# Picked k and v rows: one masked tile and four products in the edge values' bank, in place of two tiles and eight products in the query bank

## The chip, the cores and the metric

One core of one Trainium2 chip. The metric is the device time of one execution in microseconds, the median of the runs shown. Profiles are single executions taken with the hardware profiler.

## The reference

A layer of a graph network over 6250 nodes and 206250 edges, 64 channels in 4 heads of 16, and a residual layer norm behind it:

```python
Qh = (x @ Wq.T + bq).reshape(n, H, D)
Kh = (x @ Wk.T + bk).reshape(n, H, D)
Vh = (x @ Wv.T + bv).reshape(n, H, D)
Ee = (edge_attr @ We.T + be).reshape(-1, H, D)
score = (Kh[src] * Qh[dst] * (1.0 / np.sqrt(D)) * Ee).sum(-1)
score = jnp.exp(jnp.clip(score, -5.0, 5.0))
msg = Vh[src] * score[..., None]
wV = jax.ops.segment_sum(msg, dst, num_segments=n)
x = _layernorm(x + wV.reshape(n, H * D))
```

The edges are sorted by `dst`; all values are float32.

## The kernel before

A tile is 128 edges, a group 8 tiles; there are 202 groups. A first stage computes tables of k and v and of q for all nodes and writes them to DRAM. The main loop then goes over the groups, one round for each, and its order is written out by hand: within a round the instructions of each engine are queued as the code states them, and an engine takes its queue in order. The waits between engines are put in by the framework from what tiles are written and read.

In round g the parts are these. `edges(g + 3)` multiplies edge attributes with `We` into the PSUM tile `ee`. `biased(g + 2)` on ACT adds the bias and copies `ee` to SBUF as `eb`. `queries(g + 2)` puts the q of each edge into the PSUM tile `qq` by a product with a one-hot of the destinations. `terms(g + 1)` on DVE multiplies `eb` with `qq`; `turn(g + 1)` transposes the result on PE into `qe`. `products` and `weigh` make the scores of g on DVE and ACT, `message` and `keep`/`take` the messages, and `sums` (PE) adds the messages of a step of two groups into `pa`, from where `add` (DVE, L900 first) takes them a round later.

k and v of the sources come from the table by indirect DMAs on GpSimd (L295), a DMA for each tile. For two tiles of a group, of 156 groups, they are made on the core: a **batch** is four such tiles (two groups of two), and there are 78 batches. Batches last three and two groups in turn. Over a batch, `hots` (DVE, partly widened by ACT) makes one-hots of the source rows, and `picks` (PE, 50 matmuls in a batch) selects with them from all of x, held in SBUF. x lies there four nodes to a row, so that a pick bank holds two nodes' 64 channels, one in the upper and one in the lower 64 partitions: `px[0]` for the first two of the four and `px[1]` for the other two. `odd` (DVE, L259) is the source index modulo 4 and says which of the four is meant. At the end of a batch `picked` (DVE, L722 and L723) copies each bank to SBUF, masked by `odd`; the next batch's first picks write the same banks. In the round after, `biased_kv` (ACT, L733) fills the bank of `qq` with the bias, `picked_kv` (PE) adds the products of both masked tiles with `w2`, the weights of k and v, and `place_kv` (ACT, L739) copies k and v to the place where a gather would have put them. `queries(g + 2)` follows in that bank, last but one in this round's PE queue; in other rounds it stands behind `turn`.

`READY` holds the last round of each batch, `BEGIN` the first. All matmuls but the turns are issued by one helper (L744), so PE's groups are told apart by tiles. The PSUM tile `room` takes two of the eight banks: one half is `ee`, the other holds `pa` and `folded`.

Of the kernel before, what the change touches and what calls it, by code (L numbers as in the profile page):

```python
# [8 lines left out]
F32 = mybir.dt.float32  # L9
BF16 = mybir.dt.bfloat16  # L10
I32 = mybir.dt.int32
U8 = mybir.dt.uint8
# [137 lines left out]
def tile_gnn(ctx: ExitStack, tc: tile.TileContext, x, x_blocks, by_rows, xT, wT, bias, beT, weT, eT, src, src_rows,  # L150
# [502 lines left out]
    with tc.If(rv == 0) as branch:  # L653

        with tc.tile_pool(name="work", bufs=2) as work, \
# [7 lines left out]
            nc.tensor.transpose(col, row_b[:, 0:1].to_broadcast([P, P]), ident_b)  # L663
            nc.tensor.transpose(still[:, C:C + UNITS].bitcast(BF16),
                                half_b[:2 * UNITS].to_broadcast([2 * UNITS, P]), ident_b[:2 * UNITS, :2 * UNITS])
            room = fixed.tile([P, 2, 4 * P], F32, name="room")
            ee = room[:, 0].rearrange("p (i e) -> p i e", e=P)
            pa = room[:, 1, :2 * PA]
            folded = room[:, 1, 2 * PA:2 * PA + 2 * C].rearrange("p (b c) -> p b c", c=C)
            sum_ = still[:, 2 * P:2 * P + C]  # L670
            px = [fixed.tile([P, 4 * P], F32, name=f"pick{k}") for k in range(2)]
            xs = [accp.tile([P, 4 * P], F32, name=f"x{k}") for k in range(2)]
            qq = fixed.tile([P, G // 2, P], F32, name="qq")
            qe = [fixed.tile([P, G, C], F32, name=f"qe{k}") for k in range(2)]

            rooms = qq.rearrange("p i e -> p (i e)").rearrange("p (j c) -> p j c", j=BATCH)

            def pairs(ap):

# [39 lines left out]
            def picked(m):  # L719

                odd = ODD.pop(m)
                nc.vector.scalar_tensor_tensor(xs[0], odd, upper, px[0], op0=OP.is_equal, op1=OP.mult)  # L722
                nc.vector.scalar_tensor_tensor(xs[1], odd, upper2, px[1], op0=OP.is_equal, op1=OP.mult)  # L723

            def picked_kv(m):
                for j in range(BATCH):
                    for k in range(2):
                        product(rooms[:, j], xs[k][:, j * P:(j + 1) * P], w2, start=False,
                                stop=k == 1 and j == BATCH - 1, skip_group_check=True)

            def biased_kv(m):

# [10 lines left out]
            def product(*aps, **kw):  # L743
                mark.append(nc.tensor.matmul(*aps, **kw))  # L744
# [6 lines left out]
            def biased(g):  # L751

                n = tiles_of(g) // 2
                EB[g] = work.tile([P, G // 2, P], F32, name="eb")
                nc.scalar.activation(EB[g][:, :n], ee[:, :n], AF.Identity, bias=be_col)  # L755
# [258 lines left out]
            for g in range(NG + 1):  # L1014
# [37 lines left out]
                    add(s)  # L1052
                if g - 1 in FOLDS:
                    add_blocks(FOLDS[g - 1])
                if g - 1 in READY:
                    biased_kv(READY.index(g - 1))
                if g + 2 < NG:
                    biased(g + 2)
                for piece in ahead[:1]:
                    hots(*piece)  # L1060
                if now:
# [23 lines left out]
                for k in range(max(len(todo), 3)):  # L1085
                    for one in todo[k:k + 1]:
                        picks(*one)
                        where.append(mark[-1])
                    if k == 1:
                        if g + 1 < NG:  # L1090
                            turn(g + 1)
                        if g - 1 in READY:
                            picked_kv(READY.index(g - 1))
                            place_kv(READY.index(g - 1))
                        elif g + 2 < NG:
                            queries(g + 2)
                    if k in (2, 4) and short and g not in READY:
                        short.pop(0)()
                while short:
                    short.pop(0)()  # L1100
                if g + 2 < NG and g - 1 in READY:
                    queries(g + 2)
                if g + 3 < NG:
                    edges(g + 3)
                where.append(mark[-1])
# [18 lines left out]
                    take(g, 0)  # L1124
                if g in READY:
                    picked(READY.index(g))
                if done:

                    while closed < B - 2 and summed[closed] <= g:
# [192 lines left out]
```

## Time and profile before

| | |
|---|---|
| median of 3 runs | 1998.6 us (1994.48 to 2001.87) |
| the profiled execution | 2019.47 us |
| its span, first to last instruction | 2017.7 us |
| mean granted clock of TensorE | 0.932 |
| ACT busy | 1328.1 us, 66% |
| GpSimd (POOL) busy | 1255.5 us, 62% |
| DMA, mean over the span | 101 GB/s |

The profiled execution is 1% above the median of the runs. Busy times are read against the span. Names in the profile are those of tiles: `pick` the banks `px`, `qq<-w,x` the products of the picked rows, `qq<-to,qw` the query products, `room<-et` the edge products, `room<-msg` the sums, `still` the tile that holds the sum taken out.

### The profile page before, as it was taken

To read this page: it belongs to the slowest core of one execution; us is meant where nothing else is said; L and a number is where in the kernel's file an instruction comes from. 1 tells how busy PE (TensorE), PEld (TensorE's weight loads), DVE (VectorE), ACT (ScalarE), POOL (GpSimd) and SP (SyncE) were. 2 spreads that over 40 slices of the span, in tenths; PEclk is the share of its full clock that TensorE was granted. 3 is DMA by queue.
4 is the path that set the end of the run, shared out by engine and by line. 5 is a ranking of instruction groups with operands and counts; after the bars stand their busy time and mean duration, and the time that the engine had idled before them with its cause. 6 is when DMAs were issued, how large, how long until landed. Compare 5 with 4: busy or idle time off the path is not lost.

```text
span 2017.7 us, 25692 instructions
## 1 busy us (share of the span) xinstructions
PE 1738.5 (86%) x7993; PEld 1259.1 (62%) x7993; DVE 1486.0 (74%) x2650; ACT 1328.1 (66%) x2047; POOL 1255.5 (62%) x1310
## 2 busy tenths in 40 slices
PE   6569989888888898979888989888888988889995
PEld 6346666666666665657566666666666666656664
DVE  5457777777777686878777777778777777678786
ACT  3456676676766676767667667667766667577674
POOL 6566666666666665666666666666666666666441
PEclk9789999999999998999899999999989999999996
DMA  6523333333333333333333333333333333333320
GB/s 178 190 90 114 100 103 103 98 97 100 93 108 101 91 102 88 102 115 99 93 97 92 107 104 93 104 90 103 101 88 114 104 95 104 97 93 98 97 71 20
DMA packets 116116, 203.70 MB, mean 101 GB/s; under 512 B 54784, under 2 KB 56425, under 8 KB 115855
## 3 DMA queue, kind: packets, MB, share of 16 engines
q1 hardware_dynamic: 73932, 116.94, 19.0%
q0 software_dynamic: 41600, 83.97, 14.7%
q10 hardware_dynamic: 436, 1.04, 0.2%
q8 instruction: 65, 1.06, 0.2%
q14 instruction: 83, 0.68, 0.1%
HBM read 194.25 MB, written 7.59 MB: 100 GB/s over the span
## 4 chain that ended last, share of the span: by engine, by line
PE 63%; DVE 16%; issue 7%; ACT 6%; another core or an unknown queue 4%; DMA 2%; POOL 1%; DVEq 0%; SPq 0%; ACTq 0%; POOLq 0%
PE pick L744 37%; PE room L744 10%; PE qq L744 10%; PE qe L775 4%; DVE hot L696 3%; DMA kv<-kv_tab,src_i 2%; DVE score L808 2%; DVE prod L806 1%; DVE qe L830 1%; DVE x L722 1%; DVE term L769 1%; POOL kv L295 1%; ACT kv L739 1%; DVE msg L850 1%
## 5 line engine op out<-in xcount | busy, mean ns | idle before, releaser
L295 POOL DMA_INDIRECT kv<-kv_tab,src_i x1260 | 1216.2, 965 | 708.8 <-issue 277.1
L744 PE MATMUL pick<-hot,parts 128*128 128x512 f32 x3900 | 1143.6, 436 | 115.5 <-DVE x L722 79.5
L744 PEld LDWEIGHTS pick<-hot,parts 128*128 128x128 f32 x3900 | 742.3, 198 | 418.8 <-issue 167.8
L696 DVE TENSOR_TENSOR hot<-from,still 128x1024 fp32r<-128x1024 bf16 x231 | 280.3, 1213 | 0.6 <-ACT from L257 0.6
L707 ACT ACTIVATE hot<-thin 128x1024 fp32r<-128x1024 bf16 x234 | 245.4, 1049 | 19.4 <-remote 19.3
L769 DVE TENSOR_TENSOR term<-eb,qq 128x512 f32<-128x512 f32 x202 | 137.3, 680 | 137.2 <-PE qq L744 98.1
L755 ACT ACTIVATE eb<-room,be_col 128x512 f32<-128x512 f32 x202 | 137.1, 679 | 148.2 <-DVE still L900 50.4
L744 PE MATMUL room<-et,we_sb 128*128 128x512 f32 x404 | 226.2, 642 | 7.5 <-ACT eb L755 6.2
L844 ACT ACTIVATE msg<-qe 128x512 fp32r<-128x512 f32 (+1 forms) x206 | 123.2, 598 | 157.5 <-DVE qe L830 74.4
L278 ACT ACTIVATE to<-to,one_p 126x1024 bf16<-126x1024 bf16 x198 | 225.7, 1140 | 0.1
L272 ACT ACTIVATE to<-kb,minus_row 126x1024 bf16<-126x1024 uint8 x198 | 225.2, 1137 | 0.0
L813 ACT ACTIVATE score<-score,five_p 128x32 f32<-128x32 f32 x203 | 64.1, 316 | 235.4 <-DVE score L808 144.6
L775 PE MATMUL qe<-ident,term 128*128 128x128 f32 x806 | 135.5, 294 | 58.9 <-DVE term L769 39.4
L775 PEld LDWEIGHTS qe<-ident,term 128*128 128x128 f32 x806 | 104.0, 151 | 111.9 <-DVE term L769 55.8
L744 PE MATMUL qq<-w,x 128*128 128x128 f32 x1248 | 165.8, 288 | 5.0 <-issue 3.6
L806 DVE TENSOR_TENSOR prod<-kv,qe 128x512 f32<-128x512 f32 x203 | 137.0, 675 | 43.1 <-remote 38.3
L830 DVE SCALAR_TENSOR_TENSOR qe<-weight,kv 128x512 f32<-128x512 f32 x200 | 139.8, 699 | 35.1 <-ACT weight L815 22.3
L722 DVE SCALAR_TENSOR_TENSOR x<-odd,upper,pick 128x512 f32<-128x512 int32 x77 | 57.3, 744 | 144.7 <-PE pick L744 115.2
L744 PEld LDWEIGHTS qq<-w,x 128*128 128x128 f32 x1248 | 155.6, 202 | 12.9 <-issue 8.0
L696 DVE TENSOR_TENSOR thin<-from,still 128x1024 bf16<-128x1024 bf16 x231 | 157.1, 680 | 0.0
L808 DVE TENSOR_REDUCE score<-prod 128x32 f32<-128x512 f32 x203 | 138.5, 682 | 7.0
L850 DVE TENSOR_TENSOR msg<-qe,msg 128x512 fp32r<-128x512 f32 x194 | 132.2, 681 | 2.9 <-ACT msg L844 1.4
(166 smaller groups left out, 1490.5 us busy)
## 6 DMA issues: line engine op xcount, KB each, us to landing
et<-in_eT SPq DMA_DIRECT2D x100, 512.0 KB
kb<-key_tab SPq DMA_DIRECT2D x101, 252.0 KB
kv<-kv_tab,src_i POOLq DMA_INDIRECT x1260
srcs<-in_src_rows SPq DMA_DIRECT2D x78, 256.0 KB
qw<-q_tab SPq DMA_DIRECT2D x202, 15.8 KB
kv_tab<-kv_sb SPq DMA_DIRECT2D x4, 640.0 KB
q_tab<-q SPq DMA_DIRECT2D x5, 480.0 KB
out<-y SPq DMA_DIRECT2D x2, 512.0 KB
```

The source lines that it names most:

```text
L272: nc.scalar.activation(TO[g][:, :n, :], KB.pop(g)[:, :n * P].rearrange("p (j e) -> p j e", j=n), AF.Square, bias=minus_row3[:3 * W])
L278: nc.scalar.activation(TO[g][:, :n, :], TO[g][:, :n, :], AF.Relu, bias=one_p[:3 * W], scale=-1.0)
L295: return nc.gpsimd.indirect_dma_start(out=kv_of(g)[:, j, :], out_offset=None, in_=kv_tab[:, :], in_offset=bass.IndirectOffsetOnAxis(ap=src ...
L696: nc.vector.tensor_tensor(to.rearrange("p b (a c) -> p b a c", c=2), pairs((FROM if hi < UNITS else OVER)[m])[:, None].to_broadcast(shape) ...
L707: nc.scalar.activation(*THIN.pop(0), AF.Copy)
L744: mark.append(nc.tensor.matmul(*aps, **kw))
L769: nc.vector.tensor_mul(TERM[g][:, :n], EB.pop(g)[:, :n], qq[:, :n])
L775: nc.tensor.transpose(qe[g % 2][:, 2 * k:2 * k + 2, :], TERM[g][:, k, :], ident)
L806: nc.vector.tensor_mul(prod, kv_of(g)[:, lo:hi, :C], qe[g % 2][:, lo:hi, :])
L808: nc.vector.tensor_reduce(SCORE[g], prod.rearrange("p g (h d) -> p g h d", h=H), axis=AX.X, op=OP.add)
L830: nc.vector.scalar_tensor_tensor(to.rearrange("p g (h d) -> p g h d", h=H), WEIGHT.pop(g)[:, :, :, None].to_broadcast([P, n, H, D]), LEAST ...
L850: nc.vector.tensor_sub(part_of(g, 1)[1], left, part)
```

## The change

The two masked tiles become one. The first bank is copied under its mask as before, which leaves zeros where the second is meant; there the second bank is copied over it with a predicated copy, whose mask, a tile of bytes `second`, is made by a new DVE instruction in the round that begins a batch. One tile means four products with the weights, not eight. `ee` and the rest of `room` become tiles of their own, and the products of the picked rows go to `ee`'s bank, no longer to that of `qq`. For that `biased_kv` comes behind `biased(g + 2)`, which empties `ee`, and `queries(g + 2)` stands behind `turn` in every round.

```diff
-            room = fixed.tile([P, 2, 4 * P], F32, name="room")
-            ee = room[:, 0].rearrange("p (i e) -> p i e", e=P)
-            pa = room[:, 1, :2 * PA]
-            folded = room[:, 1, 2 * PA:2 * PA + 2 * C].rearrange("p (b c) -> p b c", c=C)
+            ee = fixed.tile([P, G // 2, P], F32, name="ee")
+            room = fixed.tile([P, 4 * P], F32, name="room")
+            pa = room[:, :2 * PA]
+            folded = room[:, 2 * PA:2 * PA + 2 * C].rearrange("p (b c) -> p b c", c=C)
...
-            xs = [accp.tile([P, 4 * P], F32, name=f"x{k}") for k in range(2)]
+            xs = accp.tile([P, 4 * P], F32, name="x0")
+            SECOND = {}
+
+            def second(m):
+
+                SECOND[m] = work.tile([P, BATCH * P], U8, name="second")
+                nc.vector.tensor_scalar(SECOND[m], ODD[m], upper2, None, op0=OP.is_equal)
...
-            rooms = qq.rearrange("p i e -> p (i e)").rearrange("p (j c) -> p j c", j=BATCH)
+            rooms = ee.rearrange("p i e -> p (i e)").rearrange("p (j c) -> p j c", j=BATCH)
...
-                nc.vector.scalar_tensor_tensor(xs[0], odd, upper, px[0], op0=OP.is_equal, op1=OP.mult)
-                nc.vector.scalar_tensor_tensor(xs[1], odd, upper2, px[1], op0=OP.is_equal, op1=OP.mult)
+                nc.vector.scalar_tensor_tensor(xs, odd, upper, px[0], op0=OP.is_equal, op1=OP.mult)
+                nc.vector.copy_predicated(xs, SECOND.pop(m), px[1])
...
                 for j in range(BATCH):
-                    for k in range(2):
-                        product(rooms[:, j], xs[k][:, j * P:(j + 1) * P], w2, start=False,
-                                stop=k == 1 and j == BATCH - 1, skip_group_check=True)
+                    product(rooms[:, j], xs[:, j * P:(j + 1) * P], w2, start=False, stop=j == BATCH - 1,
+                            skip_group_check=True)
...
+                if g + 2 < NG:
+                    biased(g + 2)
                 if g - 1 in READY:
                     biased_kv(READY.index(g - 1))
-                if g + 2 < NG:
-                    biased(g + 2)
...
                         if g + 1 < NG:
                             turn(g + 1)
+                        if g + 2 < NG:
+                            queries(g + 2)
                         if g - 1 in READY:
                             picked_kv(READY.index(g - 1))
                             place_kv(READY.index(g - 1))
-                        elif g + 2 < NG:
-                            queries(g + 2)
...
-                if g + 2 < NG and g - 1 in READY:
-                    queries(g + 2)
...
+                if g in BEGIN:
+                    second(BEGIN.index(g))
```

On PE, in the first round of a batch of three groups, from the last product of the picked rows (`qq<-w`) to the edge products (`room<-et`), before the change:

```order
L744 MATMUL qq<-w_100,x_760 128x128
L744 MATMUL pick_757<-hot,parts 128x512 x2
L744 MATMUL pick_758<-hot,parts 128x512 x2
L744 MATMUL pick_757<-hot,parts 128x512 x2
L744 MATMUL pick_758<-hot,parts 128x512 x2
L744 LDWEIGHTS qw [waits DMAHW6_49]
L744 MATMUL qq<-to,qw 64x512 [waits Activation_49]
L744 LDWEIGHTS qw
L744 MATMUL qq<-to,qw 64x512
L744 MATMUL room<-et,we_sb 128x512 [waits DMAHW2_49,DVE_49]
```

and in the same round of the changed kernel, from the query products to the edge products (now `ee<-et`):

```order
L749 LDWEIGHTS qw [waits DMAHW6_49]
L749 MATMUL qq<-to,qw 64x512
L749 LDWEIGHTS qw
L749 MATMUL qq<-to,qw 64x512
L749 MATMUL ee<-w_100,x_760 128x128 [waits Activation_49]
L749 MATMUL ee<-w_100,x_760 128x128 x3
L749 MATMUL pick_758<-hot,parts 128x512 x2
L749 MATMUL pick_759<-hot,parts 128x512 x2
L749 MATMUL pick_758<-hot,parts 128x512 x2
L749 MATMUL pick_759<-hot,parts 128x512 x2
L749 MATMUL ee<-et,we_sb 128x512 [waits DMAHW2_49,Activation_49]
```

The query products moved from behind eight picks to ahead of the products of the picked rows, of which there are four; the edge products, which waited for DVE, wait for ACT, and the wait of the queries for ACT is gone.

On ACT, in the same kind of round, from the fill with the bias (`qq<-bkv_all`) to the copies of k and v, before:

```order
L733 ACTIVATE qq<-bkv_all 128x512 [waits DVE_49,PE_49]
L755 ACTIVATE eb<-room,be_col 128x512 [waits DVE_49,PE_49]
L844 ACTIVATE msg<-qe_763 128x8x64 [waits DVE_49]
L272 ACTIVATE to<-kb,minus_row_86 126x1024
L707 ACTIVATE hot<-thin 128x1024 [waits DVE_49]
L739 ACTIVATE kv_68<-qq 128x256 [waits PE_49,Activation_49]
L739 ACTIVATE kv_68<-qq 128x256
```

and in the changed kernel:

```order
L760 ACTIVATE eb<-ee,be_col 128x512 [waits PE_49]
L738 ACTIVATE ee<-bkv_all 128x512 [waits Activation_49]
L849 ACTIVATE msg<-qe_763 128x8x64 [waits DVE_49]
L272 ACTIVATE to<-kb,minus_row_86 126x1024
L713 ACTIVATE hot<-thin 128x1024 [waits DVE_49]
L744 ACTIVATE kv_68<-ee 128x256 [waits PE_49,Activation_49]
L744 ACTIVATE kv_68<-ee 128x256
```

`eb` stands ahead of the fill now, and waits for PE alone; the fill waits for `eb` on its own engine, no longer for DVE and PE.

## The prediction, on record before the changed kernel ran

> **What bounds the kernel now.** I read the page from the top: busy time, then the chain that ended last, then who waits for whom, then the timeline of one batch of picks. The first lines say which engine to look at.
>
> ```profile
> span 2017.7 us, 25692 instructions
> PE 1738.5 (86%) x7993; PEld 1259.1 (62%) x7993; DVE 1486.0 (74%) x2650; ACT 1328.1 (66%) x2047; POOL 1255.5 (62%) x1310
> ...
> PE 63%; DVE 16%; issue 7%; ACT 6%; another core or an unknown queue 4%; DMA 2%; POOL 1%; DVEq 0%; SPq 0%; ACTq 0%; POOLq 0%
> PE pick L744 37%; PE room L744 10%; PE qq L744 10%; PE qe L775 4%; DVE hot L696 3%; DMA kv<-kv_tab,src_i 2%; DVE score L808 2%; DVE prod L806 1%; DVE qe L830 1%; DVE x L722 1%; DVE term L769 1%; POOL kv L295 1%; ACT kv L739 1%; DVE msg L850
> ```
>
> PE is busy for 86% of the span and carries 63% of the chain; no other engine carries more than 16%. A matmul less on PE is therefore worth close to its own time, unless something else is late at that place. The next view cuts out the main loop: a row gives length, then busy time of PE, PEld, DVE, ACT and POOL, the granted clock of TensorE, and DMA.
>
> ```profile
> 152.00:1990.00 1838.00, 1626.55 (x7610) 1177.02 (x7609) 1389.92 (x2401) 1251.07 (x1880) 1159.06 (x1203) 0.95 0.33 98
> ```
>
> In 1838 us of the loop PE is busy for 1626.55 us, so it idles for 211 us, and DVE is busy for 1389.92 us, 76%. The waits (who waited for whom, total us, times, longest) say what ends PE's idle time and what holds DVE and ACT.
>
> ```profile
> DVE term L769 <- PE qq L744: 98.1, 50, 5.1
> PE pick L744 <- DVE x L722: 79.5, 23, 6.0
> ACT eb L755 <- DVE still L900: 50.4, 20, 6.5
> PE qq L744 <- ACT kv L739: 44.0, 32, 4.4
> DVE still L900 <- PE qq L744: 41.8, 13, 6.7
> ```
>
> PE has two large waits: 79.5 us before the first pick of a batch, for the DVE instruction that empties the pick banks, and 44.0 us before the query products, for ACT to copy the picked k and v out. The other three are waits of DVE and ACT between the parts that the change moves. One batch shows them in place. Rows are start, length, engine, line, names, count, and in brackets the idle time before and its releaser.
>
> ```profile
> 975.82 0.75 DVE L722 SCALAR_TENSOR_TENSOR x<-odd,upper,pick 128x512 f32<-128x512 int32 x1 [5.14 <-PE pick L744]
> 979.98 1.96 PE L744 MATMUL qq<-w,x 128*128 128x128 f32 x16
> 981.70 2.12 PE L744 MATMUL pick<-hot,parts 128*128 128x512 f32 x8
> 984.57 0.65 ACT L739 ACTIVATE kv<-qq 128x256 f32<-128x256 f32 x2
> 985.27 0.41 PE L744 MATMUL qq<-to,qw 126*64 126x512 bf16 x2 [1.46 <-ACT kv L739]
> 985.60 1.13 PE L744 MATMUL room<-et,we_sb 128*128 128x512 f32 x2
> 986.16 2.44 PE L744 MATMUL pick<-hot,parts 128*128 128x512 f32 x8
> ...
> 991.76 0.63 PE L744 MATMUL room<-msg,wide 128*128 128x256 f32 x4
> 992.23 1.02 PE L744 MATMUL room<-et,we_sb 128*128 128x512 f32 x2
> 992.73 0.68 DVE L769 TENSOR_TENSOR term<-eb,qq 128x512 f32<-128x512 f32 x1
> 995.98 0.64 DVE L900 TENSOR_REDUCE still<-room 64x64 f32<-64x128 f32 x2 [2.56 <-PE qq L744]
> 996.71 0.69 ACT L755 ACTIVATE eb<-room,be_col 128x512 f32<-128x512 f32 x1 [2.77 <-DVE still L900]
> 1001.82 0.74 DVE L722 SCALAR_TENSOR_TENSOR x<-odd,upper,pick 128x512 f32<-128x512 int32 x1
> 1002.47 0.74 DVE L723 SCALAR_TENSOR_TENSOR x<-odd,upper,pick 128x512 f32<-128x512 int32 x1
> ```
>
> At 979.98 the eight products of the picked rows run; PE does eight more picks, and then stands for 1.46 us until ACT's copies (984.57) are done, because the queries go to the same bank. The second half shows another stall: DVE has finished its terms at 993.41 and would sum (L900), but starts at 995.98, 2.56 us later. What it sums was ready with the products that ended at 992.39 (991.76 + 0.63); it waits for the edge products too (992.23), which write the other half of the tile `room`. ACT's `eb` then waits 2.77 us for that sum. DVE reaches `x` only at 1001.82, and PE pays:
>
> ```profile
> 1002.61 3.78 PE L744 MATMUL pick<-hot,parts 128*128 128x512 f32 x8 [3.34 <-DVE x L722]
> 976.00:1002.00 26.00, 21.81 (x109) 15.88 (x107) 21.55 (x37) 17.11 (x27) 17.21 (x19) 0.99 0.37 109
> 1002.00:1024.00 22.00, 21.39 (x100) 16.32 (x100) 15.06 (x26) 15.24 (x23) 13.91 (x16) 0.86 0.35 101
> ```
>
> PE stood 3.34 us for `x`; after it eight picks took 3.78 us where they took 2.44 us at 986.16, and the granted clock was 0.86 in the 22 us from there against 0.99 in the 26 us ahead of it.
>
> **The change part by part, against the profiled execution (span 2017.7 us, 2019.47 us with what lies around it; the median of the runs shown, 1998.6 us, is 0.990 of that).**
>
> *Fewer products.* The order shows four products of the picked rows where eight stood. Each is two matmul records.
>
> ```profile
> L744 PE MATMUL qq<-w,x 128*128 128x128 f32 x1248 | 165.8, 288 | 5.0 <-issue 3.6
> ```
>
> 165.8 us busy over 78 batches are 2.13 us each (the mean of one, 288 ns, overlaps its neighbours, so I take busy time); half of it is 1.06 us a batch, 82.9 us in all. Where PE waits for nothing behind the products, that is gained whole. In the 32 batches in which it waits for ACT's copies it is not: the copies come when ACT's own chain (score, weight, `eb`, message, one-hot) comes to them, and the new order only lets PE arrive earlier. There the edge products wait in the place of the queries, and what is gained is the query products, now ahead of the gate: 985.60 - 985.27 = 0.33 us. Sum: 46 x 1.06 + 32 x 0.33 = **59 us**. The bounds: 26 us if all 78 batches are gated so, 83 us if none is.
>
> *`ee` in a tile of its own.* In the order of before, `eb` waits for DVE and PE in every other round and the edge products wait for DVE; in the changed one `eb` waits for PE alone. The sums no longer wait for the edge products. That takes away up to 2.56 us in each of the 23 waits of a pick for `x`: 59 us. But at 995.98 the release came 2.7 us after the edge products had ended by the records (992.23 + 1.02), so something else may hold DVE there too, and would hold it still. I take half, **29 us**; the bounds are 0 and 59.
>
> *The clock.* The stretch behind such a stall lost about 22 x (0.99 - 0.86) = 2.9 us. Were all 23 to go, 66 us; a shorter stall may still cost the clock, so I take a quarter, **15 us**, between 0 and 66.
>
> *The queries come ahead of the products.* In the batch that began at 1002.61 they stood last in the round:
>
> ```profile
> 1015.03 0.41 PE L744 MATMUL qq<-to,qw 126*64 126x512 bf16 x2
> 1015.55 0.69 DVE L769 TENSOR_TENSOR term<-eb,qq 128x512 f32<-128x512 f32 x1 [4.65 <-PE qq L744]
> ```
>
> DVE stood 4.65 us for them, a part of its 98.1 us for `qq`. That is no PE time, so I count nothing for it; it gives DVE the slack that hides the next item. On SP and POOL nothing moves but the gathers' release points, which are PE's marks.
>
> *`second`, a byte mask for each batch, is a new DVE instruction.* The nearest rows:
>
> ```profile
> L474 DVE TENSOR_SCALAR key_rows<-rows_i,least 112x1024 uint8<-112x1024 int32 x2 | 1.5, 772 | 0.0
> L259 DVE TENSOR_SCALAR odd<-srcs 128x512 int32<-128x512 int32 x77 | 36.9, 479 | 0.0
> L723 DVE SCALAR_TENSOR_TENSOR x<-odd,upper,pick 128x512 f32<-128x512 int32 x77 | 57.1, 741 | 0.0
> L769 DVE TENSOR_TENSOR term<-eb,qq 128x512 f32<-128x512 f32 x201 | 136.9, 681 | 137.2 <-PE qq L744 98.1 <-ACT to L278 15.4 <-ACT score L813 5.3
> 977.14 0.68 DVE L806 TENSOR_TENSOR prod<-kv,qe 128x512 f32<-128x512 f32 x1
> 977.86 0.69 DVE L808 TENSOR_REDUCE score<-prod 128x32 f32<-128x512 f32 x1
> ```
>
> L474 has its form (int32 in, a scalar by partition, bytes out): 772 ns for 1024 elements, so 386 ns for 512 at least; L259 on 512 takes 479 ns. I take 0.45 us, 35 us of DVE in 78 batches. It stands at the end of the round that begins a batch, ahead of the next product with kv; the wait for `qq` that the queries lose covers it. Where DVE is what PE waits for it is not covered: 23 x 0.45 = **10 us** lost; the bounds are 0 and 35.
>
> *The copy under the mask takes the place of the second x.* No row shows this operation. Below stands `term`, two tensors with one in PSUM, 681 ns; the instruction it replaces, L723, takes 741 ns; above I put twice that, 1482 ns, for an operation that would also read what it keeps. I take 0.74 us, nothing won or lost; the bounds are +5 and -58 us (78 x 0.74). What is new is that it waits for the first x on its own engine. L723 starts 0.65 us after L722, which has 0.74 us (1002.47 and 1001.82), so the two overlap by 0.09 us; the score, which waits for the product on its own engine, starts 0.72 us after it, 0.04 us more than the product's 0.68. With the lost overlap that is 0.13 us a batch, **10 us**, between 0 and 10: the second pick bank comes free so much later, and behind it stands the next batch's first pick into it. The page "VectorE: DVE Perf Modes" of the Trainium skill, section "The DRAIN you can't avoid", says that chaining without semaphores saves nothing, which would make this 0; the rows disagree by the 0.13 us.
>
> The sum is -59 - 29 - 15 + 10 + 10 = -83 us: 2019.5 - 83 = 1936.5 in a profiled execution, times 0.990 gives **1917 us**.
>
> **The rivals.**
>
> *The copies gate every batch.* ACT is 1251 us busy in the loop, so it has room, but its chain hangs on `x`, and faster products make PE arrive earlier everywhere. Then the first term is 26 us; with half of the next, 29 us, and 20 us lost it is -35: 1984, times 0.990, 1964 us. For it: 32 batches wait already, the longest 4.4 us. Against it: in a batch of two groups 16 picks follow the products, not the eight shown, and 46 batches have no such wait. If the 29 us stay away as well, it is -6 us, 1993 us, no change that can be told.
>
> *DVE comes free altogether.* All of the sums' wait and all of the clock: -59 - 59 - 66 + 20 = -164, 1836 us. For it: the shared tile is the only thing that the order shows between 992.39 and 995.98. Against it: the late release, and that even an `x` 2.56 us earlier would leave PE 3.34 - 2.56 = 0.8 us.
>
> *The copy under the mask is slow.* It stands between the last pick of one batch and the first of the next into the same bank, where PE has only sums and edge products to do (0.63 us for four sums, 1.02 us for the edges), so that each microsecond more costs 78 us. From 0.74 + 83/78 = 1.8 us on the change is lost; at 2.4 us it would be 78 x 1.66 = 129 us, -83 + 129 = +46, 2044 us. For it only that no row shows it; against it that the rows of 512 elements above lie between 0.48 and 0.74 us.
>
> *The wait becomes long enough for the clock.* PE with less to do waits longer for the copies: 1.46 + 0.73 = 2.2 us in the batch shown, up to 4.4 + 0.7 = 5.1. A stall of 3.34 us was followed by a loss of 2.9 us; if all 32 were, +93 - 83 = +10, 2009 us. The batch with 1.46 us was followed by no such loss (0.99), so I give it little. The page "TensorE: Matmul & The Clock Gate" of the Trainium skill, section "What's actually happening", puts the halving of the clock behind an idle window of about 3.4 us; by that rule a wait of 2.2 us is safe, and the rows here agree, 3.34 us with and 1.46 us without.
>
> That the change doesn't do what it says is excluded by the order: four rows, one x.
>
> **How the numbers follow.** The forecast (1875 to 1950 us) has 0.62; DVE comes free, below 1875, 0.14; the copies gate, 1950 to 1988, 0.12, and within 0.5% of 1998.6, 0.05; slower, 0.07, of which the slow copy has 0.04 and the clock 0.03. 0.5%, 10 us, is about what a measurement of this kernel can tell from no change. Faster by more is 0.62 + 0.14 + 0.12 = 0.88. For 8 in 10 the range takes some of the neighbours on both sides, 0.09 each: 1850 to 1975 us. Each bound by itself lies within: the copy at twice its time gives 1974, the clock given back whole 1867; all on one side at once I leave out.
>
> **What would show it.** Right: matmuls of the picked rows at half their busy time; no wait of `eb` for the sums; fewer waits of picks for `x`; edge products waiting for ACT's copies in some 30 batches; a copy under the mask of 0.7 us; a granted clock above 0.93. Wrong: PE's wait for the copies well over 44 us, or picks that wait for the copy under the mask in all 78 batches. The forecast falls if DVE still waits 2 to 3 us ahead of the sums, or if ACT's copies come later than now, since ACT now does `eb` ahead of filling the bank.

## The result, and the profile after

| | before | changed |
|---|---|---|
| median, 7 runs each | 1999.85 us (1994.48 to 2003.54) | 1987.26 us (1982.49 to 1992.88) |
| ratio, 95% interval | | 0.9934 (0.9916 to 0.9952) |
| the profiled execution | 2019.47 us | 1987.82 us |

The change gains 0.7%, 13 us, and not the 4% of the prediction. The kernel before takes 1785 to 1786 us in some of the sets of runs that follow and 1997 to 2018 us in others, on one and the same chip in two sets twelve minutes apart; these are called the **short** and the **long level** below, and the first comparison was at the long one. Each ratio is against runs of the kernel before in the same set, on the same chip.

The page of the changed kernel, its span, its busy times and the chain that ended last:

```profile
span 1986.0 us, 24370 instructions
...
PE 1665.1 (84%) x7369; PEld 1180.0 (59%) x7369; DVE 1515.3 (76%) x2728; ACT 1321.2 (67%) x2047; POOL 1258.1 (63%) x1310
...
PE 52%; DVE 24%; issue 9%; ACT 7%; another core or an unknown queue 5%; DMA 1%; POOL 1%; DVEq 0%; SPq 0%; ACTq 0%; POOLq 0%
```

The main loop (same columns as in the prediction):

```profile
152.00:1960.00 1808.00, 1556.99 (x7007) 1101.32 (x7005) 1421.91 (x2483) 1246.43 (x1885) 1163.66 (x1205) 0.94 0.35 100
```

PE did 73 us less (1738.5 before), and the loop became 30 us shorter in this pair of profiles. So more than half of what PE was spared turned into idle time, and PE's share of the chain fell from 63% to 52%. The groups, by form: busy time, mean ns, idle time ahead and what ended it.

```profile
L749 PE MATMUL ee<-w,x 128*128 128x128 f32 x624 | 92.8, 293 | 19.8 <-ACT ee L738 11.4 <-issue 6.7 <-ACT eb L760 1.7
...
L905 DVE TENSOR_REDUCE still<-room 64x64 f32<-64x128 f32 x194 | 57.9, 298 | 95.4 <-PE pick L749 40.0 <-PE qq L749 30.3 <-PE room L749 8.8
L728 DVE SCALAR_TENSOR_TENSOR x<-odd,upper,pick 128x512 f32<-128x512 int32 x77 | 57.4, 745 | 199.9 <-PE pick L749 85.4 <-remote 61.4 <-issue 18.4
L729 DVE COPY_PREDICATED x<-second,pick 128x512 f32<-128x512 uint8 x78 | 57.1, 733 | 11.6 <-DVE x L728 1.6 <-issue 1.4 <-remote 1.3
...
L678 DVE TENSOR_SCALAR second<-odd,upper 128x512 uint8<-128x512 int32 x77 | 38.0, 494 | 0.0
```

and the two groups on DVE as they were before the change:

```profile
L900 DVE TENSOR_REDUCE still<-room 64x64 f32<-64x128 f32 x194 | 58.0, 299 | 87.8 <-PE qq L744 41.8 <-PE pick L744 17.0 <-PE room L744 8.6
L722 DVE SCALAR_TENSOR_TENSOR x<-odd,upper,pick 128x512 f32<-128x512 int32 x77 | 57.3, 744 | 144.7 <-PE pick L744 115.2 <-remote 29.5
```

The products, the copy under the mask (733 ns) and the mask (494 ns) cost what the prediction said within 10 us. But `still` (L905, which was L900) still idles 95.4 us, 87.8 before, although the edge products no longer stand in its way; and x (L728) now idles 199.9 us, 144.7 before, of which 61.4 have a releaser that the profile can't name (29.5 before). The waits:

```profile
PE pick L749 <- DVE x L728: 107.6, 29, 8.0
...
DVE still L905 <- PE pick L749: 40.0, 23, 4.8
...
PE ee L749 <- ACT kv L744: 39.3, 27, 2.5
```

The picks wait longer for x than before (79.5 us, 23 times). The timeline shows how. First the middle of the last round of a batch of three groups:

```profile
979.61 0.64 PE L749 MATMUL room<-msg,wide 128*128 128x256 f32 x4
...
980.09 1.02 PE L749 MATMUL ee<-et,we_sb 128*128 128x512 f32 x2
...
983.69 2.65 PE L749 MATMUL pick<-hot,parts 128*128 128x512 f32 x10
...
986.44 0.63 DVE L905 TENSOR_REDUCE still<-room 64x64 f32<-64x128 f32 x2 [4.81 <-PE pick L749]
...
986.48 0.69 ACT L760 ACTIVATE eb<-ee,be_col 128x512 f32<-128x512 f32 x1 [4.33 <-PE pick L749]
...
992.28 0.74 DVE L728 SCALAR_TENSOR_TENSOR x<-odd,upper,pick 128x512 f32<-128x512 int32 x1
...
993.07 3.78 PE L749 MATMUL pick<-hot,parts 128*128 128x512 f32 x8 [4.73 <-DVE x L728]
```

The sums end at 980.25 by the record (979.61 + 0.64), and DVE, which wants only them, stands 4.81 us, to 986.44. The page puts the wait down to a pick, which is merely PE's latest row. ACT's `eb` is let go at the same moment. DVE then has 5.8 us of work ahead of x, and PE stands 4.73 us. The end of another such batch:

```profile
1033.22 2.60 PE L749 MATMUL pick<-hot,parts 128*128 128x512 f32 x10
...
1035.65 1.12 PE L749 MATMUL room<-msg,wide 128*128 128x256 f32 x8
1036.61 1.02 PE L749 MATMUL ee<-et,we_sb 128*128 128x512 f32 x2
...
1041.27 0.75 DVE L728 SCALAR_TENSOR_TENSOR x<-odd,upper,pick 128x512 f32<-128x512 int32 x1 [5.56 <-remote]
...
1042.07 3.78 PE L749 MATMUL pick<-hot,parts 128*128 128x512 f32 x8 [4.44 <-DVE x L728]
```

The last pick ends at 1035.82 (1033.22 + 2.60), DVE is free, and x starts at 1041.27 with an unnamed releaser. Between 1037.63 and 1041.27 no row of PE, DVE or ACT runs. In the trace all 77 rows of x (L728) wait for one semaphore alone, that of PE, so that the mask, `odd` or a DMA can't be what x waits for.

The page "Perfetto Trace Analysis" of the Trainium skill, section "Tensor Engine Instruction (MATMUL, LD_WEIGHTS)", says that the end of a matmul in a trace is an estimate from its size, and that the update which releases others goes out later, once PSUM has acknowledged the writes. The trace agrees that the two can part, by up to 8.7 us here.

So I measured this **lateness** in each trace: for every x, sum (`still`), `eb`, copy of k and v, product with k and term, its start less the later of two times, the end of the instruction ahead of it on its engine and the recorded end of the last matmul of the group on which it depends. Cases over 0.6 us, in us (from 150 us after the start to 60 us before the end):

| kernel, level | x | sums | eb | k, v | product, term | all |
|---|---|---|---|---|---|---|
| before, long | 29.5 | 69.0 | 104.1 | 60.3 | 21.5 | 284 |
| changed, long | 84.6 | 69.5 | 53.8 | 29.4 | 6.5 | 244 |
| before, short | 0 | 4.8 | 36.5 | 0 | 0 | 41 |
| changed, short | 0 | 0 | 0 | 0 | 0 | 0 |

The 41 us of the kernel before at the short level are the shared tile (sums behind edge products, `eb` behind sums); with the tile split and nothing else, the first experiment, they are 0. At the long level some 240 us more are there in both kernels. In the changed one more of it falls on x (84.6 us in place of 29.5), for which PE waits. The same measure for ACT's score behind DVE's score stays at 0.04 us on both levels: PE's completions come late, those of DVE don't.

The trace's own records of semaphore updates say the same. In the first timeline above, ten PE rows that update PE's semaphore end between 980.25 and 986.10, but the trace records two updates in that time (984.21 and 984.94), and then five within 0.22 us, from 986.36 to 986.58, at which the sum and `eb` start. Over the whole run of the changed kernel, 506 of the 1703 steps from one recorded PE update to the next are 70 ns or less; at the short level it is 16 of 2216. All 104 late starts come within 0.15 us of a recorded PE update. So PE's updates come out late and in bursts, which speaks against DVE or ACT being slow to act on them.

### The profile page after: what moved, and what is told of

It reads as the page before. It is cut to its first block, busy times and chain, and to the rows that moved or that the text cites. A ratio compares the mean times of both kernels' runs of the same rounds, so it can differ in the third digit from the quotient of the medians.

```text
span 1986.0 us, 24370 instructions
## 1 busy us (share of the span) xinstructions
PE 1665.1 (84%) x7369; PEld 1180.0 (59%) x7369; DVE 1515.3 (76%) x2728; ACT 1321.2 (67%) x2047; POOL 1258.1 (63%) x1310
## 4 chain that ended last, share of the span: by engine, by line
PE 52%; DVE 24%; issue 9%; ACT 7%; another core or an unknown queue 5%; DMA 1%; POOL 1%; DVEq 0%; SPq 0%; ACTq 0%; POOLq 0%
PE pick L749 32%; PE ee L749 8%; DVE hot L702 5%; PE room L749 4%; PE qe L780 3%; PE qq L749 3%; DVE x L728 2%; DVE prod L811 2%; DVE qe L835 2%; DVE score L813 2%; DVE msg L855 2%; DVE thin L702 2%; DVE still L905 1%; DMA kv<-kv_tab,src_i 1%
## 5 line engine op out<-in xcount | busy, mean ns | idle before, releaser
L749 PE MATMUL ee<-et,we_sb 128*128 128x512 f32 x404 | 218.6, 623 | 46.4 <-ACT kv L744 39.3
L728 DVE SCALAR_TENSOR_TENSOR x<-odd,upper,pick 128x512 f32<-128x512 int32 x77 | 57.4, 745 | 199.9 <-PE pick L749 85.4
L760 ACT ACTIVATE eb<-ee,be_col 128x512 f32<-128x512 f32 x202 | 135.8, 672 | 88.7 <-PE pick L749 33.8
L813 DVE TENSOR_REDUCE score<-prod 128x32 f32<-128x512 f32 x203 | 138.5, 682 | 7.0
L905 DVE TENSOR_REDUCE still<-room 64x64 f32<-64x128 f32 x194 | 57.9, 298 | 95.4 <-PE pick L749 40.0
L749 PEld LDWEIGHTS room<-msg,wide 128*128 128x128 f32 x776 | 114.3, 191 | 25.0 <-issue 11.3
```

Source lines behind the costliest of these rows:

```text
L813: nc.vector.tensor_reduce(SCORE[g], prod.rearrange("p g (h d) -> p g h d", h=H), axis=AX.X, op=OP.add)
```

## The experiments

Theory of the first set: at these places PE's completions are late by themselves, so that neither the tile nor all of the PE time was on the path (the path is the chain of work that sets the time). Rival: the prediction's terms are right and something new (the mask, the order, the bank) takes them back. This set fell on the short level (before 1785.56 us).

**`ee` in a tile of its own, nothing else.** The first hunk of the diff alone, in the kernel before.

> The kernel before, with `ee` and the rest of `room` as tiles of their own and nothing else changed. The prediction's term (the tile shared by edge products and sums makes DVE, and so x and the picks, late): -29 us of 2000, ratio to before 0.985. Rival (in these rounds PE's completions reach DVE late by themselves, so the wait of DVE ahead of the sums stays): ratio 0.997 to 1.003, and the wait of `still` L900 for PE stays near its 88 us.

1773.64 us, ratio 0.9932 (0.9920 to 0.9944): 12 us gained, between the two expectations. The wait ahead of the sums for the edge products is gone. Its group in the kernel before at this level (a later run, below), and here:

```profile
L900 DVE TENSOR_REDUCE still<-room 64x64 f32<-64x128 f32 x194 | 57.8, 298 | 20.6 <-PE room L744 17.2
```

```profile
L900 DVE TENSOR_REDUCE still<-room 64x64 f32<-64x128 f32 x194 | 57.4, 296 | 3.8 <-PE room L744 0.4
```

**The products twice.** Each of the four products is issued twice.

```diff
-                    product(rooms[:, j], xs[:, j * P:(j + 1) * P], w2, start=False, stop=j == BATCH - 1,
-                            skip_group_check=True)
+                    for k in range(2):
+                        product(rooms[:, j], xs[:, j * P:(j + 1) * P], w2, start=False,
+                                stop=k == 1 and j == BATCH - 1, skip_group_check=True)
```

> The changed kernel with each of the four products of the picked rows issued twice into the same place, so that the picked k and v are wrong and all else is as it was. If PE time of the products is paid whole in every batch: the products' busy time goes back up by about 73 us, ratio to before 1.030. If it is paid in the 39 batches of two groups only, where PE has little idle time: 39 x 0.94 = 37 us, ratio 1.012. If it is hidden (DVE or a late completion sets the pace): 0.993, as the change itself.

1782.69 us, 0.9983 (0.9974 to 0.9992).

**The mask twice.** `for _ in range(2):` ahead of the instruction that makes `second`.

> The changed kernel with the byte mask `second` made twice in each batch. If DVE sets the pace and the mask is paid whole: 78 x 0.494 = 38 us more, ratio to before 1.012. If it is paid in the 39 batches of three groups only: 19 us, 1.003. If the mask lies beside other work: 0.993.

1757.72 us, 0.9837 (0.9824 to 0.9849).

**Eight products in the new place.** The changed kernel with two masked tiles and eight products, as before:

```diff
...
-                nc.vector.scalar_tensor_tensor(xs, odd, upper, px[0], op0=OP.is_equal, op1=OP.mult)
-                nc.vector.copy_predicated(xs, SECOND.pop(m), px[1])
+                nc.vector.scalar_tensor_tensor(xs[0], odd, upper, px[0], op0=OP.is_equal, op1=OP.mult)
+                nc.vector.scalar_tensor_tensor(xs[1], odd, upper2, px[1], op0=OP.is_equal, op1=OP.mult)
...
-                if g in BEGIN:
-                    second(BEGIN.index(g))
```

> The changed kernel's places and order (own tile for `ee`, products in its bank, queries behind the turn), but the two masked tiles and eight products of before, and no byte mask. If one tile and four products are worth their PE time (73 us) less mask and wait on the own engine (at most 20 to 48 us): ratio to before 1.005 to 1.02, so that the move of the bank by itself costs time. If the move gives the gain and the four products none (their time comes back as later completions): 0.99 to 0.995.

1772.85 us, 0.9929 (0.9917 to 0.9942), the same as the tile alone: bank and order bring nothing, at no cost. That is in the second expected range; its reading, that the four products gain nothing, falls with the next run. The changed kernel itself had to be run at this level; so the second set (short level, before 1786.48 us).

> The changed kernel once more. In the first comparison (before 1999.9 us) DVE's x started over 1 us after the recorded end of the last pick in 19 batches; in the four experiments, on a chip where before takes 1785.6 us, in none. If those late completions of PE ate the gain: where before takes about 1786 us the ratio is 0.972 to 0.980 (mask made twice is 0.984, eight products 0.993), and where before takes about 2000 us it is 0.993 again. If the gain is small for another reason that lies in the program: 0.990 to 0.995 on either chip.

1743.66 us, 0.9766 (0.9752 to 0.9779): **2.3%, 43 us**, in place of 0.7%. The ratios expected of the first set had been counted from 0.993, which the change has at the long level alone. Counted from 0.9766, doubled products cost 39 us, of the 62 us of PE time that they add at this level (1648.8 us busy against 1587.0). Batches of three and of two groups come in two kinds each, beginning on an even or an odd group; from one x to the next, the batches get longer by 0 and 0.88 us in the two kinds of three groups and by 0.87 and 0.36 us in those of two, so the cost is not in those of two alone.

> The kernel before, for a profile from the same chip as the experiments. Late completions: x starts over 1 us behind the last pick in none of the batches where before takes about 1786 us, against 6 in the profile at 2017.7 us; PE idle in batches of three groups falls from 2.8 and 4.5 us to below 2 us. If the program alone makes these gaps they are as in the first profile.

No x starts late there, and PE idles 1.44 and 1.66 us in the two kinds of batches of three groups, which are 23.2 and 24.2 us long (25.2 and 27.2 in the first profile). Its page and waits:

```profile
span 1784.7 us, 25692 instructions
...
PE 1658.4 (93%) x7993; PEld 1207.1 (68%) x7993; DVE 1480.7 (83%) x2650; ACT 1322.4 (74%) x2047; POOL 1250.7 (70%) x1310
```

```profile
PE qq L744 <- ACT kv L739: 24.9, 19, 1.5
ACT eb L755 <- DVE still L900: 21.6, 14, 2.1
...
PE pick L744 <- DVE x L722: 16.8, 20, 1.7
```

and the changed kernel at this level, page, waits and the end of a batch of three groups:

```profile
span 1741.9 us, 24370 instructions
...
PE 1587.0 (91%) x7369; PEld 1135.3 (65%) x7369; DVE 1508.3 (87%) x2728; ACT 1315.4 (76%) x2047; POOL 1258.8 (72%) x1310
```

```profile
PE ee L749 <- ACT kv L744: 35.7, 35, 1.8
...
PE ee L749 <- ACT ee L738: 19.5, 67, 0.3
PE pick L749 <- DVE x L728: 18.1, 19, 1.9
```

```profile
1086.62 2.61 PE L749 MATMUL pick<-hot,parts 128*128 128x512 f32 x10
...
1089.07 1.02 PE L749 MATMUL ee<-et,we_sb 128*128 128x512 f32 x2
...
1090.29 0.73 DVE L728 SCALAR_TENSOR_TENSOR x<-odd,upper,pick 128x512 f32<-128x512 int32 x1
...
1091.08 2.51 PE L749 MATMUL pick<-hot,parts 128*128 128x512 f32 x8 [0.98 <-DVE x L728]
```

Here x follows its own engine's queue, at 1090.29, and PE stands 0.98 us, where it stood 4.44 us at the long level.

**The mask left out.** A tile of zeros, filled once, in the place of `second`.

> The changed kernel with the byte mask set to zeros once, ahead of the loop, so that the second bank is never copied over and the picked k and v of half the nodes are wrong; 78 DVE instructions of 494 ns are gone. If DVE sets the pace in all batches: 38 us less than the changed kernel, 2.2%. If only where x waits for DVE (the three-group batches, 39 of 78): 19 us, 1.1%. If the mask lies beside other work: nothing, within 0.3%.

1740.64 us, 0.9742 (0.9727 to 0.9757): 3 us less than the changed kernel, with intervals that overlap. So the mask lies beside other work, while a second one costs 13 us (0.9837 against 0.9766).

Third set: is a late x enough to take the gain away? Nine idle DVE instructions ahead of x in batches of three groups, in both kernels, and a reordering that looked better. This set fell on the long level (before 2018.47 us), so the stall came on top of the lateness.

```diff
...
+                    if READY[m] - BEGIN[m] == 2:
+                        for _ in range(9):
+                            idle = work.tile([P, BATCH * P], U8, name="idle", bufs=1)
+                            nc.vector.tensor_scalar(idle, ODD[m], upper2, None, op0=OP.is_equal)
...
```

> The kernel before, with nine DVE instructions of some 0.49 us, which write a tile that nothing reads, ahead of `x` at the end of each of the 39 batches of three groups: x comes some 4.5 us later there. If PE has nothing else to do, 39 x 4.5 = 175 us are added to 1786, 1.098, and half-clock stretches come back behind the stalls (7 stretches of 73 us without them, 42 of 278 us in the first profile of this kernel at 2017.7 us). If the stalls are taken up by slack of DVE, below 1.04.

> The changed kernel with the same nine DVE instructions at the same places. Theory: a late x takes away what PE saved in that batch, because PE only waits longer for it; the gain stays in the batches of two groups (0.73 us in two of them, 14 us over the run) and the 1.47 us of two batches of three groups, 28 us, is gone: the ratio of this kernel to before_stalled is 0.99 to 0.995, near the 0.993 of the first comparison. Rival: PE's saving is paid in any case, 42 us: 0.976 to 0.980.

2113.81 us (1.0487, 1.0458 to 1.0516) and 2080.63 us (1.0335, 1.0292 to 1.0378). The stall costs the kernel before 95 us, neither of the two figures expected, which had been counted from the short level. The change is worth 33 us, 1.6%, here, between theory and rival. Where it comes from fits the theory: the two kinds of batches of two groups shrink by 0.51 and 1.14 us, those of three groups grow by 0.17 and 0.31. That is 1.17 us in four batches, some 22 of the 33 us; the rest isn't placed. The size is off: 1.65 us in two batches of two groups, where the expectation had 0.73 from the short level. With DVE late anyway, lateness at x is 1.4 and 8.8 us and in all 135 and 121, half of what it is without the stall, and the change gains 1.6% where it gained 0.7%.

**ACT's copies first.** In the round behind `READY`, `place_kv` ahead of `onehot_rows(g + 4)` and the last widening.

> The changed kernel with ACT's two copies of the picked k and v ahead of two longer instructions (one-hot of the destinations, widening of a one-hot of the sources) in the round that takes a batch out. The edge products wait 35.7 us in 35 rounds for these copies. If that wait is on the path: up to 36 us less than the changed kernel, ratio to before 0.957 to 0.970. If DVE, or ACT's work that now comes later, sets the pace there: 0.975 to 0.980, as the changed kernel.

2006.89 us, 0.9947 (0.9930 to 0.9964), and once more in the last set 1990.95 us, 0.9960 (0.9935 to 0.9984). That run's expectation:

> The kernel of copies_first once more, for the other condition. Where before takes about 1786 us: up to 36 us below the changed kernel, ratio 0.957 to 0.970, if the edge products' wait for the copies is on the path, and 0.975 to 0.980 if DVE or ACT sets the pace. At 2000 us or more: 0.995 again.

No gain at the long level: 166 and 122 us of lateness now fall on the copies themselves. What it does at the short level was not seen.

Fourth set, long level (before 2017.79 us): the parts of the change against each other, and one test of what the lateness is.

> The changed kernel once more, beside the next three. If before takes about 1786 us here: 0.977 again. If it takes 2000 us or more (as in the first comparison and the last one): 0.990 to 0.996, with consumers of PE's results (x, sums, eb, k and v) starting over 0.6 us behind the recorded end of what they wait for, together some 200 us, and x with the most of it.

> The kernel before with `ee` in a tile of its own, once more. About 1786 us: 0.993 again. At 2000 us or more: if the tile shared by sums and edge products holds DVE there (the prediction's term), 0.985; if PE's late completions hold it, 0.997 to 1.003.

> The changed kernel with its four products issued twice, so that the picked k and v are wrong. About 1786 us: 0.998 again, 39 us more than the changed kernel. At 2000 us or more: if PE time saved comes back as later completions, no more than 15 us over the changed kernel; if the products are paid whole, 60 us or more.

2007.37 us, 0.9943 (0.9921 to 0.9964); 2017.56 us, 0.9994 (0.9980 to 1.0008); 2018.60 us, 1.0002 (0.9988 to 1.0016). At this level the tile is worth nothing, and all of the change but the halved products, the mask with it, is worth nothing together; the halving has the whole gain, 2018.6 - 2007.4 = 11 us. In the kernel with the tile alone no edge product can hold DVE, and yet:

```profile
PE pick L744 <- DVE x L722: 84.0, 23, 6.1
...
DVE still L900 <- PE qq L744: 30.9, 11, 3.1
...
DVE still L900 <- PE pick L744: 19.2, 8, 4.5
```

**Fewer picks.** The eight picks of the low parts of x are left out in the last round of each batch of three groups.

```diff
+                last = READY[m] - BEGIN[m] == 2 and p >= len(PIECES) * 2 // 3
...
-                    for part in range(2 if u < UNITS - 1 else 1):
+                    for part in range(2 if u < UNITS - 1 and not last else 1):
```

> The changed kernel without the eight picks of the low parts of x in the last round of each batch of three groups (so these values are wrong): 39 x 8 matmuls, 39 x 2.44 = 95 us of PE time less, just ahead of `x`. If PE is behind its records by work that it has not done yet (a backlog), x comes earlier by the whole of it and by the lag: at 2000 us or more 80 us or more less than the changed kernel, and the lag of x behind the last pick falls to half of its 84.6 us. If the late completion is an event apart from the amount of work, the lag stays as it is and most of the 95 us turns into waiting: less than 50 us. About 1786 us DVE takes over there: 20 to 50 us less than the changed kernel.

2006.03 us, 0.9946 (0.9925 to 0.9967): nothing gained over the changed kernel's 2007.37. Lateness is 262 us, at x 71 (258 and 98 in the changed kernel of this set). PE was busy 56 us less (1669.8 us in that kernel), less than the 95 expected, while time at half clock rose from 310 to 361 us; and PE stood longer for x, 138.5 us where that kernel has 119.1:

```profile
PE 1614.1 (81%) x7057; PEld 1129.6 (56%) x7057; DVE 1516.0 (76%) x2728; ACT 1321.5 (66%) x2047; POOL 1253.5 (63%) x1310
```

```profile
PE pick L750 <- DVE x L729: 138.5, 31, 7.9
```

So most of the lateness isn't work that PE still has to do: with less work ahead of it, the whole stays and the part at x falls by a quarter, not by half. Once more in the last set (before 1996.95 us), with the same outcome: 1986.65 us, 0.9945 (0.9920 to 0.9970).

> The kernel of fewer_picks once more, for the other condition. Where before takes about 1786 us: 95 us of PE work less in the batches of three groups; if PE sets the pace there, 1743 - 95 = 1648 us, ratio 0.923; if DVE takes over (22.4 us busy of 24.1 in such a batch), 1695 to 1725 us, 0.950 to 0.966; if nothing is gained even there, 0.977. At 2000 us or more: 0.995 again.

**PE kept busy.** The edge products repeated five times at the end of each batch of three groups.

> The changed kernel with the edge products repeated five times (the same values into the same bank) at the end of each batch of three groups, ahead of the next batch's first pick: 39 x 5 x 1.02 = 199 us more of PE work, placed where PE waits for `x`. At 2000 us or more: if the half-clock stretches and the late completions come from PE's standing idle there, both shrink (under 150 us at half clock against 310, x late by under 30 us in all against 85), and the time falls by 50 us or more below the changed kernel; if the completions are late whatever PE does, the time stays within 15 us of it, since the added work lies in the wait. About 1786 us, where PE waits 0.5 to 2.3 us in such a batch: 100 to 180 us more than the changed kernel.

The first run fell on the short level: 1838.37 us, 1.0302 (1.0284 to 1.0319), 95 us more than the changed kernel, a little under what was expected. The run in the last set fell on the long one:

> The kernel of kept_busy once more. Where before takes about 1786 us: 1.030 again. At 2000 us or more: if half clock and late completions come from PE's standing idle ahead of x, 0.97 or below, with under 150 us at half clock; if the completions are late whatever PE does, 0.99 to 1.00.

2002.50 us, 1.0024 (1.0004 to 1.0043): 390 added matmuls cost 0.8% beside the changed kernel's 0.9943 in the fourth set, 16 us, just outside the range expected if the completions are late whatever PE does. Half-clock time fell to 158 us (310 in the changed kernel of the fourth set), but x is late by 95.5 us, as ever, and nothing is won. PE's wait for x is filled, DVE's wait for PE is not:

```profile
DVE x L728 <- PE pick L749: 86.6, 33, 4.3
...
DVE x L728 <- PE ee L749: 57.5, 11, 7.5
...
PE pick L749 <- DVE x L728: 13.2, 9, 2.2
```

Together: at the long level 312 picks fewer bring nothing and 390 edge products more cost 16 us, while the lateness stays between 244 and 314 us in every kernel without the added stall. PE time in the batches of three groups is nearly free there.

## Why the prediction was wrong, step by step

| term | predicted | long level | short level |
|---|---|---|---|
| fewer products | -59 | -11 by doubling them | -39 by doubling them |
| mask, copy, wait on the own engine | +20 | about 0 (1.0002, with the tile, bank and order) | +10 (29 of those 39 are left) |
| `ee` in a tile of its own | -29 | -1 (0.9994) | -12 (0.9932) |
| bank and order | 0 | in the above | 0 (0.9929 against 0.9932) |
| the clock | -15 | 0 (279 us at half clock, 278 before) | 0 (71 us, 73 before) |
| all | -83 | -13 | -43 |

**What failed first is the opening step**, that a matmul less "is therefore worth close to its own time, unless something else is late at that place". PE's share of the chain, 63%, was read as PE working. At the long level DVE stands for completions that come up to 8.7 us behind PE's recorded ends, and of the 70 us that PE was spared in the loop 40 became idle time. The trace of the kernel before held the sign: 284 us of lateness over 119 places.

**The tile** was where the prediction came closest to this. It saw the release 2.7 us behind the end of the edge products, said that something else might hold DVE there, and took half. The other half should have gone too: with the tile alone the long level gains 1 us. The prediction's own test, "the forecast falls if DVE still waits 2 to 3 us ahead of the sums", came true: 95.4 us in all, up to 4.8 us at a time.

**The products** were mis-sized even where nothing is late. The fair pair is the changed kernel with its products doubled and the changed kernel, both at the short level, which differ in nothing else:

```profile
PE 1648.8 (92%) x7993; PEld 1206.9 (68%) x7993; DVE 1511.9 (85%) x2728; ACT 1315.9 (74%) x2047; POOL 1261.2 (71%) x1310
```

```profile
PE ee L750 <- ACT ee L739: 18.9, 67, 0.3
...
PE ee L750 <- ACT kv L745: 14.0, 19, 0.8
```

PE is busy 62 us less with four products (1587.0), where the prediction had 83 (half the busy time of their group at the long level). Ahead of the edge products it stands 35.7 us for ACT's copies in place of 14.0, so 22 us of the 62 came back as a wait; the prediction had taken off 24 for it (83 - 59). That makes 40 us, near the 39 us of the doubled products: the step that was off is the PE time, and the wait was priced right. The new wait of 19.5 us for ACT's fill of the bank, since ACT does `eb` first, is there with eight products too (18.9 us); it comes with the order and is no loss of the halving.

**The clock** was to be won by shorter stalls. At the long level the stalls stayed (24 gaps of PE over 3 us from 152 to 1960 us, 23 before) and so did the time at half clock, 279 us against 278. The run that kept PE busy halved that time and still gained nothing, though with 390 matmuls more to do; no run here shows a gain from less time at half clock at the long level.

**The mask and the copy** were right: 494 and 733 ns against 450 and 740, and with the wait on the own engine 10 us at the short level where 20 were put down. The rival that the copies gate every batch did not come (27 waits, 39.3 us), though its 1964 to 1993 us take in the 1987 measured: its number is right here by luck. Nor did the slow copy come (733 ns), nor DVE coming free altogether (95.4 us ahead of the sums), nor waits for the copies long enough for the clock (the longest is 2.5 us). Of the signs named ahead, halved products, no wait of `eb` for the sums, some 30 waits for the copies and a copy of 0.7 us came true; fewer waits of picks for x and a granted clock above 0.93 (it is 0.930) did not.

**Open:** what makes PE's completions late and come in bursts at the long level, and what sets the level. The runs speak against work left on PE (fewer picks, in the main), the shared tile (tile alone), PE standing idle ahead of x and the half clock behind that (PE kept busy), and a property of the chip (one chip showed both). That the lost gain sits in this lateness rests on its place (the sums, x), on its absence where the gain is 2.3%, on the stalled pair, where it is half as large and the gain 1.6%, and on the runs that move PE's work and hardly the time; a run that takes the lateness alone away wasn't tried, so that this is argued and not shown.

## What to carry to other kernels

Before pricing PE time that a change saves, compare the recorded ends of matmuls with the starts of what they release: here, with consumers that had a free engine and started microseconds late in about 100 places, saved matmuls were worth little, whatever PE's busy share. Ask of every wait that a change removes what the next latest release is, and by how much it came later than its own record. And time before and after next to each other, since the same kernel moved by 13% within twelve minutes, and the worth of one change is 2.3% at one level and 0.7% at the other.

## What was not expected of the hardware

- Two levels of the same program: 1786 and 1997 to 2018 us. DVE, ACT and GpSimd are busy for the same time on both, within 0.5% in the profiles of the kernel before (the copy under the mask takes 735 and 733 ns in those of the changed one); what differs there is the lateness of PE's completions, 41 and 284 us, the time at half clock, 73 and 278 us, and PE's busy time, 1658 and 1738 us.
- The traces of the long level hold far fewer semaphore updates: 11344 for the kernel before against 35553 for the same program at the short level. Of 2167 rows that update PE's semaphore, 1717 left a record of the update at the long level and 2165 at the short one. Whether updates came merged or records were lost, the traces don't tell.
- At the long level 390 more matmuls of 512 columns, at the places where PE waits, cost 16 us; at the short level 95 us.
